# Layer 0's preparation: channel halves added before the averages, and the gate's second convolution in fours

## The chip, the cores and the metric

The kernel runs on one core of a Trainium2 chip. The metric is the device time of one launch in microseconds (us). The runs of the kernel before gave a median of 4865.72 us (4865.72 to 4866.03, three runs).

A core has five engines that work side by side, each through its own instructions in order: TensorE (PE, matmuls), VectorE (DVE), ScalarE (ACT), GpSimd (POOL), and SyncE (SP), which here only issues transfers. They wait for each other by semaphores. PE writes its results to PSUM, in banks of 128 partitions x 512 float32; the other data lie in SBUF, 128 partitions wide.

## What is computed

Two attention layers run one after the other on an image x of shape (2, 256, 64, 64): two batches, 256 channels, N = 4096 positions. Only the start of the first layer is touched. Cut to what matters:

```python
xf = x.reshape(B, C, N).transpose(0, 2, 1)
mu = mean(xf, axis=-1)                        # over the 256 channels
var = mean(square(xf - mu), axis=-1)
xn = (xf - mu) * rsqrt(var + LN_EPS) * norm_w + norm_b
q, k, v = split(einsum('bnc,oc->bno', xn, qkv_w))      # 4 heads of 16
attn = softmax(q k^T * 16**-0.5)
d1 = relu(einsum('oc,bchw->bohw', conv1_w, x) + conv1_b)   # 128 channels
dyn = einsum('oc,bchw->bohw', conv2_w, d1) + conv2_b       # 1 channel: the gate
out = (attn * dyn) v, projected by out_w
x1 = sigmoid(gamma * out + x)
```

The second layer is attention over x1 with 4 heads of 64, a projection, biases and the sum with x1.

## The kernel before

All products are in float32. The 256 channels are two halves of 128 partitions (CC = 2), so a tile of x is 128 x 2 x 512. A block is one such tile: 512 positions of one batch, and there are 16 of them (2 batches x 8).

The kernel has three large stages: the preparation of layer 0 for all blocks (the loop at L527), layer 0's main loop over 256 steps of scores, exponentials and weighted values, and layer 1. The preparation is what concerns us. Its loop runs over n = 0 to 18, and three blocks are in work at once: new (block n), middle (block n-1) and old (block n-2). The order in which one turn writes down its work is:

- prep_load (L264): x of blocks n and n+1, if it is not there already. These transfers are not bound to the order written down; they are issued as soon as one of the four buffers of x is free, and a buffer is freed by the first convolution of its block (prep_gate).
- prep_var (L287) of middle: two matmuls with mean_w, a 128 x 128 matrix filled with 1/256, one for each half of the squares, added up in a PSUM bank. Every partition then holds the variance. prep_std (L294) takes the root on ACT.
- prep_mean (L268) of new: two matmuls with the same matrix on the halves of x.
- prep_rstd (L299) of middle: the reciprocals on DVE, in four pieces of 128 columns, two before and two after the next step.
- prep_center (L276) of new: DVE subtracts the mean (xc), ACT squares it (sq).
- prep_norm (L303) of middle: three instructions on POOL, the product with the reciprocal and, for each half, scale and shift.
- first_maxima: four score matmuls of 32 x 128 (L394, tile a) whose row maxima DVE takes (L398); this is done twice in a turn, from n = 3 on, with four PSUM banks of its own.
- prep_product and prep_keep of old: q and k (L258, tile p), copied out by ACT.
- prep_gate of middle: the first convolution (L258, tile d1p), then ACT's relu into d1.
- prep_values (L335) of old: eight matmuls of 128 columns (L340, tile vp), and ACT's copy.
- prep_dyn (L363) of middle: one matmul with c2, a column of 128 weights, to one row of a bank (L365, tile dynp); prep_keep_dyn (L370) adds the bias on ACT into a 1 x 512 row and stores that row to the memory dyn0, from which the main loop later loads it for the block.

Nearly all of these are wrapped in `seq`, which keeps the order written down on every engine. Not wrapped are transfers, the constants, and fill_wpad (L134), six small DVE copies that lay out the q, k, v weights: these may be placed anywhere that their inputs allow. The preparation's products take their PSUM banks from four in rotation (prep_bank). clear_v (L242) zeroes v of one batch on POOL and writes its columns of ones, in turn 0 for batch 0 and in turn 6 for batch 1.

```python
for c in range(CC):                                   # prep_var
    seq(nc.tensor.matmul(ps, mean_w, sq[:, c, :], start=(c == 0), stop=(c == CC - 1)))
```

Of the kernel before, what the change touches and what calls it, by code (L numbers as in the profile page):

```python
# [8 lines left out]
F32 = mybir.dt.float32  # L9
BF16 = mybir.dt.bfloat16  # L10
AF = mybir.ActivationFunctionType
ALU = mybir.AluOpType
# [3 lines left out]
P = 128  # L16
NB = 512
C = 256
CC = C // P
# [8 lines left out]
def conv_attention_kernel(  # L28
# [19 lines left out]
    nc = tc.nc  # L48
    B, _, N = x.shape
# [17 lines left out]
    const_prep = own_prep.enter_context(tc.tile_pool(name="const_prep", bufs=1))  # L67
# [7 lines left out]
    dyn0 = [  # L75
        [dram.tile([1, NB], F32, tag=f"dyn0_{b}_{j}", name=f"dyn0_{b}_{j}") for j in range(NJ)]
        for b in range(B)
    ]
# [7 lines left out]
    def load_x(b, j, pool=xpool, tag="x"):  # L86
        t = pool.tile([P, CC, NB], F32, tag=tag, name=f"{tag}_{b}_{j}")
        nc.sync.dma_start(
            out=t, in_=x[b, :, bass.ts(j, NB)].rearrange("(c p) n -> p c n", p=P)
        )  # L90
        return t

    xs = {(0, 0): load_x(0, 0)}

    def const_load(shape, src, name, pool=const):
        t = pool.tile(shape, F32, tag=name, name=name)
        nc.scalar.dma_start(out=t, in_=src)
        return t
# [7 lines left out]
    c1 = const_load([P, CC, P], c1_wT.rearrange(by_chunk, p=P), "c1", const_prep)  # L106
    c1b = const_load([P, 1], c1_b, "c1b", const_prep)
    c2 = const_load([P, 1], c2_wT, "c2", const_prep)
    c2b = const_load([1, 1], c2_b, "c2b", const_prep)


    mean_w = const_prep.tile([P, P], F32, tag="mean_w", name="mean_w")
# [19 lines left out]
    make_identity(nc, ident)  # L132

    def fill_wpad():  # L134
        for s in range(3):
            for c in range(CC):
                nc.vector.tensor_copy(
                    wpad[s][:, c, :].rearrange("p (h e) -> p h e", e=32)[:, :, 1 : 1 + D0],
                    qkv_raw[:, c, s * H * D0 : (s + 1) * H * D0].rearrange(
                        "p (h d) -> p h d", d=D0  # L140
                    ),
                )
# [67 lines left out]
    seq = tc.keep_in_program_order  # L210
# [22 lines left out]
    with own0:  # L233
        prep = own_prep.enter_context(tc.tile_pool(name="prep", bufs=2))
# [7 lines left out]
        def clear_v(b):  # L242

            seq(nc.gpsimd.memset(vs0[b], 0.0))
            ones_at = vs0[b].rearrange("p m (h e) -> p m h e", e=32)[:, :, :, 0:1]
            seq(nc.gpsimd.memset(ones_at, 1.0))

        work, qs0, mxs, pts, avs, dyns, res, facts = {}, {}, {}, {}, {}, {}, {}, {}
# [4 lines left out]
        def prep_bank(name):  # L253
            return psw.tile([P, NB], F32, tag="bank", name=name)
# [9 lines left out]
        def prep_load(b, j):  # L264
            if (b, j) not in xs:
                xs[b, j] = load_x(b, j)

        def prep_mean(b, j):  # L268
            ps = prep_bank(f"mean_{b}_{j}")
            for c in range(CC):  # L270
                seq(nc.tensor.matmul(
                    ps, mean_w, xs[b, j][:, c, :], start=(c == 0), stop=(c == CC - 1)
                ))
            work["mean", b, j] = ps

        def prep_center(b, j):  # L276
            xc = prep.tile([P, CC, NB], F32, tag="xc", bufs=3, name=f"xc_{b}_{j}")
            sq = prep.tile([P, CC, NB], F32, tag="sq", bufs=1, name=f"sq_{b}_{j}")
            mean = work.pop(("mean", b, j))
            seq(nc.vector.tensor_tensor(  # L280
                xc, xs[b, j], mean.unsqueeze(1).to_broadcast([P, CC, NB]), ALU.subtract
            ))
            seq(nc.scalar.activation(sq, xc, AF.Square))
            work["xc", b, j] = xc
            work["sq", b, j] = sq

        def prep_var(b, j):  # L287
            ps = prep_bank(f"var_{b}_{j}")
            sq = work.pop(("sq", b, j))
            for c in range(CC):  # L290
                seq(nc.tensor.matmul(ps, mean_w, sq[:, c, :], start=(c == 0), stop=(c == CC - 1)))  # L291
            work["var", b, j] = ps

        def prep_std(b, j):  # L294
            std = prep.tile([P, NB], F32, tag="std", name=f"std_{b}_{j}")
            seq(nc.scalar.activation(std, work.pop(("var", b, j)), AF.Sqrt, bias=eps))
            work["std", b, j] = std

        def prep_rstd(b, j, i):  # L299
            std = work["std", b, j]  # L300
            seq(nc.vector.reciprocal(std[:, bass.ts(i, P)], std[:, bass.ts(i, P)]))
# [53 lines left out]
        def prep_gate(b, j):  # L355
            work["d1", b, j] = over_channels(prep_bank(f"d1p_{b}_{j}"), c1, xs.pop((b, j)))

        def prep_keep_gate(b, j):
            d1 = prep.tile([P, NB], F32, tag="d1", name=f"d1_{b}_{j}")
            seq(nc.scalar.activation(d1, work["d1", b, j], AF.Relu, bias=c1b))  # L360
            work["d1", b, j] = d1

        def prep_dyn(b, j):  # L363
            ps = prep_bank(f"dynp_{b}_{j}")
            seq(nc.tensor.matmul(  # L365
                ps[:1, :], c2, work.pop(("d1", b, j)), start=True, stop=True
            ))
            work["dyn", b, j] = ps

        def prep_keep_dyn(b, j):  # L370
            row = prep.tile([1, NB], F32, tag="dyn", name=f"dynrow_{b}_{j}")
            seq(nc.scalar.activation(
                row, work.pop(("dyn", b, j))[:1, :], AF.Identity, bias=c2b
            ))
            nc.sync.dma_start(out=dyn0[b][j], in_=row)

        def load_q(u):
            b, j = u
# [6 lines left out]
        def maxima(x, g):  # L385

            u = b, j = units0[x // NM]
            m, i = divmod(x % NM, PB)
            if u not in mxs:
                mxs[u] = small.tile([P, PB * H, NJ], F32, tag="mx0", name=f"mx0_{b}_{j}")  # L390
            for h in (2 * g, 2 * g + 1):
                r = slice(32 * h, 32 * h + 32)
                ps = bank(f"a0_{b}_{j}_{x % NM}_{h}")
                seq(nc.tensor.matmul(  # L394
                    ps, qs0[u][r, bass.ts(i, P)], kTs[b][r, bass.ts(m, NB)],
                    start=True, stop=True,
                ))
                seq(nc.vector.tensor_reduce(mxs[u][:, i * H + h, m : m + 1], ps, AX.X, ALU.max))  # L398
# [127 lines left out]
        blocks = [(b, j) for b in range(B) for j in range(NJ)]  # L526
        for n in range(len(blocks) + 3):  # L527

            def block(k):
                return blocks[n - k] if 0 <= n - k < len(blocks) else None  # L530

            def first_maxima(i):
                x = 2 * (n - 3) + i
                if 0 <= x < NM:
                    for g in (1, 0):
                        maxima(x, g)

            new, middle, old = block(0), block(1), block(2)
            if n == 0:
                clear_v(0)  # L540
            if n == 6:
                clear_v(1)
            if new is not None:
                prep_load(*new)
                if block(-1) is not None:
                    prep_load(*block(-1))
            if middle is not None:
                prep_var(*middle)
                prep_std(*middle)
            if new is not None:  # L550
                prep_mean(*new)
            if middle is not None:
                prep_rstd(*middle, 0)
                prep_rstd(*middle, 1)
            if new is not None:
                prep_center(*new)
            if n == 0:
                fill_wpad()
            if middle is not None:
                prep_rstd(*middle, 2)  # L560
                prep_rstd(*middle, 3)
                prep_norm(*middle)
            first_maxima(0)
            if old is not None:
                for s in range(2):
                    prep_product(*old, s)
                    prep_keep(*old, s)
            if middle is not None:
                prep_gate(*middle)
                prep_keep_gate(*middle)  # L570
            first_maxima(1)
            if old is not None:
                prep_values(*old)
                prep_keep_values(*old)
            if middle is not None:
                prep_dyn(*middle)
                prep_keep_dyn(*middle)
        own_prep.close()
        own_psum.close()
        own_psum = ExitStack()  # L580
# [48 lines left out]
    with (  # L629
# [389 lines left out]
        for n, u in enumerate(units):  # L1019
            b, g, j = u  # L1020
            t0 = n * US
            if n == 0:
                for i in range(NJ):
                    with_x(
                        t0 + KEYS_AT[i], "early", ("k", b, g, i), b, i,
                        lambda xt, b=b, g=g, i=i: keys(b, g, i, xt),
# [4 lines left out]
                        lambda xt, b=b, g=g, i=i: values(b, g, i, xt),  # L1031
# [142 lines left out]
        for j in range(NJ):  # L1174
            project_half(j, 1, last_att[0][:, bass.ts(j, NB)])
            nc.sync.dma_start(
                out=out[B - 1, :, bass.ts(j, NB)].rearrange("(c p) n -> p c n", p=P),
                in_=last_x[j],
# [50 lines left out]
```

## Time and profile before

| what | value |
|---|---|
| median of three runs | 4865.72 us |
| the profiled execution's own time | 4865.83 us |
| its span, first to last instruction | 4864.0 us |
| mean granted TensorE clock | 0.993 |
| preparation's first turns, until PE is busy without a gap | 0 to 35.59 us |
| preparation, to the last product of v | 238.5 us |
| first exponential of layer 0's main loop | 257.2 us |

One execution was recorded by the hardware profiler. A view gives for each group of instructions its line (L291 is line 291 of the kernel), its engine, what it writes and reads with the shape, a count, and its busy time; in brackets may stand how long the engine was idle before it, and on whom it waited. The chain of waits is followed back from the last instruction of the span, at each step to what released it; read in order of time it tells which engine set the pace in each stretch. Each float32 matmul shows as two records, and the ends of matmuls in a list overlap a little, since they are pipelined; the chain counts each piece of time once.

### The profile page before, as it was taken

To read this page: it belongs to the slowest core of one execution; us is meant where nothing else is said; L and a number is where in the kernel's file an instruction comes from. 1 tells how busy PE (TensorE), PEld (TensorE's weight loads), DVE (VectorE), ACT (ScalarE), POOL (GpSimd) and SP (SyncE) were. 2 spreads that over 40 slices of the span, in tenths; PEclk is the share of its full clock that TensorE was granted. 3 is DMA by queue.
4 is the path that set the end of the run, shared out by engine and by line. 5 is a ranking of instruction groups with operands and counts; after the bars stand their busy time and mean duration, and the time that the engine had idled before them with its cause. 6 is when DMAs were issued, how large, how long until landed. Compare 5 with 4: busy or idle time off the path is not lost.

```text
span 4864.0 us, 70477 instructions
## 1 busy us (share of the span) xinstructions
PE 4608.3 (95%) x27592; PEld 1517.7 (31%) x27592; DVE 3949.3 (81%) x4614; ACT 3418.6 (70%) x4547; POOL 2524.5 (52%) x1463
## 2 busy tenths in 40 slices
PE   9999999999999999879999999999999999999997
PEld 3433333333333333223232323222333333222222
DVE  5677777777777777218999999999998899999996
ACT  3356666666666666547888888888887788888884
POOL 3200000000000000007999999999998889999995
PEclk9999999999999999989999999999999999999999
DMA  3100000000000000021000110000102111100002
GB/s 96 38 1 16 14 14 14 14 17 14 14 14 16 21 12 12 7 67 55 22 25 22 41 40 25 22 24 27 55 27 63 49 56 40 31 7 14 14 18 70
DMA packets 105195, 139.57 MB, mean 29 GB/s; under 512 B 43742, under 2 KB 44574, under 8 KB 104750
## 3 DMA queue, kind: packets, MB, share of 16 engines
q1 hardware_dynamic: 103220, 134.61, 9.2%
q8 instruction: 216, 3.54, 0.3%
q14 instruction: 117, 0.96, 0.1%
q10 hardware_dynamic: 1642, 0.46, 0.0%
HBM read 93.33 MB, written 41.45 MB: 28 GB/s over the span
## 4 chain that ended last, share of the span: by engine, by line
PE 54%; POOL 18%; DVE 14%; issue 7%; ACT 6%; DMA 1%; ACTq 0%; POOLq 0%; DVEq 0%; SPq 0%
PE s L427 23%; POOL acc L878 16%; PE av L442 11%; DVE rmax L788 8%; PE s L771 5%; DVE raw L854 5%; ACT raw L789 3%; PE av L888 3%; ACT raw L866 2%; PE a L394 1%; POOL acc L876 1%; PE p L258 1%; PE k1p L670 1%; PE o L489 1%; PE var L291 1%
## 5 line engine op out<-in xcount | busy, mean ns | idle before, releaser
L878 POOL TENSOR_TENSOR acc<-acc,raw 128x1024 f32<-128x1024 f32 x886 | 2101.5, 2372 | 104.5 <-ACT raw L866 44.7
L398 DVE TENSOR_REDUCE mx<-a 128x1 f32<-128x512 f32 x2048 | 1311.6, 684 | 433.4 <-PE a L394 432.7
L430 ACT ACTIVATE p<-s 128x512 f32<-128x512 f32 x2048 | 1111.5, 595 | 725.6 <-PE s L427 371.6
L427 PE MATMUL s<-q,kT 32*128 32x512 f32 x4096 | 1252.4, 640 | 22.9 <-ACT p L430 22.9
L854 DVE TENSOR_TENSOR raw<-raw,shift 128x1024 f32<-128x1024 f32 x1024 | 1236.6, 1212 | 16.6 <-PE shift L849 9.6
L788 DVE TENSOR_TENSOR rmax<-s,rmax 128x1024 f32<-128x1024 f32 x960 | 1169.3, 1218 | 97.7 <-PE s L771 96.4
L771 PE MATMUL s<-q,k 64*128 64x512 f32 x4096 | 1111.7, 635 | 131.3 <-ACT raw L789 123.3
L789 ACT COPY raw<-s 128x1024 f32<-128x1024 f32 x1024 | 1036.1, 1012 | 270.1 <-DVE rmax L788 180.9
L866 ACT ACTIVATE raw<-raw 128x1024 f32<-128x1024 f32 x1024 | 1085.4, 1061 | 172.8 <-DVE raw L854 139.7
L394 PE MATMUL a<-kT,q 32*128 32x512 f32 x4096 | 1123.6, 643 | 1.4 <-DVE mx L398 1.3
L888 PE MATMUL av<-raw,v 128*64 128x512 f32 x4096 | 1000.4, 607 | 4.4 <-ACT raw L866 2.5
L483 POOL TENSOR_TENSOR f<-f,dyn 128x512 f32<-128x512 f32 x16 | 20.2, 1263 | 1444.9 <-ACT p L430 1294.7
L442 PE MATMUL av<-p,v 128*32 128x256 f32 (+1 forms) x7904 | 646.4, 399 | 0.0
L771 PEld LDWEIGHTS s<-q,k 64*128 64x128 f32 x4096 | 316.9, 185 | 810.1 <-ACT raw L789 609.4
L427 PEld LDWEIGHTS s<-q,kT 32*128 32x128 f32 x4096 | 403.9, 183 | 484.5 <-issue 366.2
L888 PEld LDWEIGHTS av<-raw,v 128*64 128x64 f32 x4096 | 243.6, 136 | 585.9 <-issue 423.4
L442 PEld LDWEIGHTS av<-p,v 128*32 128x32 f32 x7904 | 156.0, 108 | 748.6 <-issue 737.8
L394 PEld LDWEIGHTS a<-kT,q 32*128 32x128 f32 x4096 | 301.7, 184 | 29.7 <-DVE mx L398 17.5
L504 POOL TENSOR_SCALAR res<-res 128x1024 f32<-128x1024 f32 x16 | 16.7, 1045 | 400.5 <-ACT res L503 400.5
L876 POOL TENSOR_TENSOR acc<-raw,raw 128x1024 f32<-128x1024 f32 x64 | 152.2, 2378 | 99.4 <-ACT raw L866 99.4
L479 DVE RECIPROCAL f<-f 128x128 f32<-128x128 f32 x64 | 59.6, 939 | 96.2 <-ACT f L475 96.2
L808 DVE TENSOR_REDUCE negs<-rt 128x4 f32<-128x512 f32 x128 | 88.2, 689 | 50.3 <-PE rt L796 47.9
(323 smaller groups left out, 1946.1 us busy)
## 6 DMA issues: line engine op xcount, KB each, us to landing
x<-in_x_dram SPq DMA_DIRECT2D x16, 512.0 KB
res<-in_x_dram SPq DMA_DIRECT2D x16, 512.0 KB
x<-res SPq DMA_DIRECT2D x16, 512.0 KB
att<-rows SPq DMA_DIRECT2D x62, 128.0 KB
kd<-k1s SPq DMA_DIRECT2D x24, 256.0 KB
vd<-v1s SPq DMA_DIRECT2D x24, 256.0 KB
k<-kd SPq DMA_DIRECT2D x24, 256.0 KB
v<-vd SPq DMA_DIRECT2D x24, 256.0 KB
```

What stands on the lines that cost most here:

```text
L394: seq(nc.tensor.matmul(ps, qs0[u][r, bass.ts(i, P)], kTs[b][r, bass.ts(m, NB)], start=True, stop=True,))
L398: seq(nc.vector.tensor_reduce(mxs[u][:, i * H + h, m : m + 1], ps, AX.X, ALU.max))
L427: seq(nc.tensor.matmul(ps, kTs[b][r, bass.ts(m, P)], qs0[u][r, :], start=True, stop=True))
L430: seq(nc.scalar.activation(pt[:, k, :], ps, AF.Exp, scale=D0**-0.5))
L442: seq(nc.tensor.matmul(avs[u][32 * h : 32 * h + 32, cols], vs0[b][:, m, 32 * h : 32 * h + 32], pts[t, h // 2][:, h % 2, cols], start=(m == ...
L771: seq(nc.tensor.matmul(ps[:, k, :], ks[b, g, m // PB][r, bass.ts(m % PB, P)], qs1[u][r, :], start=True, stop=True,))
L788: seq(nc.vector.tensor_tensor(rmax[u, n], ps, before, ALU.max))
L789: seq(nc.scalar.copy(raw, ps))
L854: seq(nc.vector.tensor_tensor(raws[t], raws[t], shifts[u, t % NM // GS], ALU.add))
L866: seq(nc.scalar.activation(p, p, AF.Exp, scale=D1**-0.5))
L878: seq(nc.gpsimd.tensor_tensor(accs[u, n], accs[u, n], p, ALU.add))
L888: seq(nc.tensor.matmul(avs1[u, n][k * D1 : (k + 1) * D1, :], v[:, m % PB, k, :], raws[t][:, k, :], start=(m % GS == 0), stop=(m % GS == GS ...
```

## The change

The two halves of the channels are added elementwise before the average is taken, so that one matmul with mean_w gives the mean, and one the variance. A new function, prep_sum, adds the halves of x into a tile of 128 x 512, on POOL at the end of the turn before the block is new, and for block 0 on DVE in turn 0. prep_center adds the two halves of the squares on POOL, after ACT's Square.

The second convolution is no longer done for each block. Its weight column is repeated 32 times (c2rep, a DVE copy in fill_wpad), and in the turns n = 4, 8, 12 and 16 four blocks are done at once: four matmuls of 128 x 32, each to its own 32 partitions of one PSUM bank. One ACT instruction adds the bias to all 128 partitions, and four transfers store one row each. For this the tile d1 has five buffers instead of two, and the bias c2b is loaded to all partitions. The zeroing of v for batch 0 moves from turn 0 to turn 1.

```diff
--- before.py
+++ after.py
@@ -106,7 +106,8 @@
     c1 = const_load([P, CC, P], c1_wT.rearrange(by_chunk, p=P), "c1", const_prep)
     c1b = const_load([P, 1], c1_b, "c1b", const_prep)
     c2 = const_load([P, 1], c2_wT, "c2", const_prep)
-    c2b = const_load([1, 1], c2_b, "c2b", const_prep)
+    c2b = const_load([P, 1], c2_b.partition_broadcast(P), "c2b", const_prep)
+    c2rep = const_prep.tile([P, 32], F32, tag="c2rep", name="c2rep")
 
 
     mean_w = const_prep.tile([P, P], F32, tag="mean_w", name="mean_w")
@@ -132,6 +133,7 @@
     make_identity(nc, ident)
 
     def fill_wpad():
+        nc.vector.tensor_copy(c2rep, c2.to_broadcast([P, 32]))
         for s in range(3):
             for c in range(CC):
                 nc.vector.tensor_copy(
@@ -265,12 +267,16 @@
             if (b, j) not in xs:
                 xs[b, j] = load_x(b, j)
 
+        def prep_sum(b, j, engine=nc.gpsimd):
+
+            x = xs[b, j]
+            both = prep.tile([P, NB], F32, tag="both", name=f"both_{b}_{j}")
+            seq(engine.tensor_tensor(both, x[:, 0, :], x[:, 1, :], ALU.add))
+            work["both", b, j] = both
+
         def prep_mean(b, j):
             ps = prep_bank(f"mean_{b}_{j}")
-            for c in range(CC):
-                seq(nc.tensor.matmul(
-                    ps, mean_w, xs[b, j][:, c, :], start=(c == 0), stop=(c == CC - 1)
-                ))
+            seq(nc.tensor.matmul(ps, mean_w, work.pop(("both", b, j)), start=True, stop=True))
             work["mean", b, j] = ps
 
         def prep_center(b, j):
@@ -281,14 +287,15 @@
                 xc, xs[b, j], mean.unsqueeze(1).to_broadcast([P, CC, NB]), ALU.subtract
             ))
             seq(nc.scalar.activation(sq, xc, AF.Square))
+            squares = prep.tile([P, NB], F32, tag="squares", name=f"squares_{b}_{j}")
+            seq(nc.gpsimd.tensor_tensor(squares, sq[:, 0, :], sq[:, 1, :], ALU.add))
             work["xc", b, j] = xc
-            work["sq", b, j] = sq
+            work["sq", b, j] = squares
 
         def prep_var(b, j):
             ps = prep_bank(f"var_{b}_{j}")
             sq = work.pop(("sq", b, j))
-            for c in range(CC):
-                seq(nc.tensor.matmul(ps, mean_w, sq[:, c, :], start=(c == 0), stop=(c == CC - 1)))
+            seq(nc.tensor.matmul(ps, mean_w, sq, start=True, stop=True))
             work["var", b, j] = ps
 
         def prep_std(b, j):
@@ -356,23 +363,22 @@
             work["d1", b, j] = over_channels(prep_bank(f"d1p_{b}_{j}"), c1, xs.pop((b, j)))
 
         def prep_keep_gate(b, j):
-            d1 = prep.tile([P, NB], F32, tag="d1", name=f"d1_{b}_{j}")
+            d1 = prep.tile([P, NB], F32, tag="d1", bufs=5, name=f"d1_{b}_{j}")
             seq(nc.scalar.activation(d1, work["d1", b, j], AF.Relu, bias=c1b))
             work["d1", b, j] = d1
 
-        def prep_dyn(b, j):
-            ps = prep_bank(f"dynp_{b}_{j}")
-            seq(nc.tensor.matmul(
-                ps[:1, :], c2, work.pop(("d1", b, j)), start=True, stop=True
-            ))
-            work["dyn", b, j] = ps
-
-        def prep_keep_dyn(b, j):
-            row = prep.tile([1, NB], F32, tag="dyn", name=f"dynrow_{b}_{j}")
-            seq(nc.scalar.activation(
-                row, work.pop(("dyn", b, j))[:1, :], AF.Identity, bias=c2b
-            ))
-            nc.sync.dma_start(out=dyn0[b][j], in_=row)
+        def prep_dyn(four):
+
+            ps = prep_bank("dynp_{}_{}".format(*four[0]))
+            for i, u in enumerate(four):
+                seq(nc.tensor.matmul(
+                    ps[32 * i : 32 * i + 32, :], c2rep, work.pop(("d1", *u)),
+                    start=True, stop=True,
+                ))
+            rows = prep.tile([P, NB], F32, tag="dyn", bufs=1, name="dynrows_{}_{}".format(*four[0]))
+            seq(nc.scalar.activation(rows, ps, AF.Identity, bias=c2b))
+            for i, (b, j) in enumerate(four):
+                nc.sync.dma_start(out=dyn0[b][j], in_=rows[32 * i : 32 * i + 1, :])
 
         def load_q(u):
             b, j = u
@@ -536,7 +542,7 @@
                         maxima(x, g)
 
             new, middle, old = block(0), block(1), block(2)
-            if n == 0:
+            if n == 1:
                 clear_v(0)
             if n == 6:
                 clear_v(1)
@@ -544,6 +550,8 @@
                 prep_load(*new)
                 if block(-1) is not None:
                     prep_load(*block(-1))
+            if n == 0:
+                prep_sum(*new, nc.vector)
             if middle is not None:
                 prep_var(*middle)
                 prep_std(*middle)
@@ -572,9 +580,10 @@
             if old is not None:
                 prep_values(*old)
                 prep_keep_values(*old)
-            if middle is not None:
-                prep_dyn(*middle)
-                prep_keep_dyn(*middle)
+            if middle is not None and n % 4 == 0:
+                prep_dyn(blocks[n - 4 : n])
+            if block(-1) is not None:
+                prep_sum(*block(-1))
         own_prep.close()
         own_psum.close()
         own_psum = ExitStack()
```

## The prediction

> **What bounds the kernel now.** I read the page's header, then its chain of waits, then asked for that chain in order of time over the preparation, which is the only stage that the diff touches.
>
> ```profile
> span 4864.0 us, 70477 instructions
> PE 4608.3 (95%) x27592; PEld 1517.7 (31%) x27592; DVE 3949.3 (81%) x4614; ACT 3418.6 (70%) x4547; POOL 2524.5 (52%) x1463
> ```
>
> TensorE is busy 95% of the whole span, but that is a mean over several stages. The busy time of the engines by stage says more:
>
> ```profile
> 0.00:35.59 35.59, 24.72 (x57) 10.22 (x57) 11.67 (x17) 10.60 (x13) 16.75 (x37) 0.90 0.57 167
> 35.59:49.64 14.05, 14.05 (x55) 6.21 (x55) 9.33 (x13) 4.70 (x7) 3.87 (x3) 1.00 0.27 83
> 49.64:218.25 168.61, 168.61 (x649) 74.55 (x649) 111.91 (x156) 56.38 (x84) 50.12 (x38) 1.00 0.16 51
> 218.25:230.81 12.56, 12.56 (x54) 5.68 (x54) 8.21 (x12) 3.71 (x6) 3.86 (x3) 1.00 0.06 21
> 230.81:258.00 27.19, 25.01 (x101) 12.87 (x104) 18.74 (x31) 4.42 (x7) 0.00 (x0) 0.75 0.03 11
> ```
>
> Columns: stretch, its length, then busy time of PE, weight loads, DVE, ACT, POOL, then the granted clock. From 35.59 to 230.81 PE is busy for the entire stretch; DVE has 9.33 of 14.05 us, POOL 3.87. So this stage is PE alone, and its chain shows only PE, in a period of 14.05:
>
> ```profile
> 91.79 1.91 PE var L291 x4
> 93.70 1.72 PE mean L271 x4
> 95.42 1.07 PE a L394 x8
> 96.49 3.63 PE p L258 x8
> 100.12 1.72 PE d1p L258 x4
> 101.84 1.07 PE a L394 x8
> 102.91 1.98 PE vp L340 x16
> 104.89 0.95 PE dynp L365 x2
> 105.84 1.91 PE var L291 x4
> ```
>
> The counts are records, two to a matmul: mean is two matmuls, 0.86 us each. The same shape costs 1.72 after itself and 1.91 after dynp, so leaving the 1-column product costs 0.19. One more view, the timeline of one period (beginning at S = 105.84), gives the other engines:
>
> ```profile
> 108.57 1.76 DVE L301 RECIPROCAL std<-std 128x128 f32<-128x128 f32 x2 [3.16 <-ACT std L296]
> 110.25 1.16 DVE L280 TENSOR_TENSOR xc<-x,mean 128x1024 f32<-128x1024 f32 x1
> 111.33 1.75 DVE L301 RECIPROCAL std<-std 128x128 f32<-128x128 f32 x2
> 113.00 2.41 DVE L398 TENSOR_REDUCE mx<-a 128x1 f32<-128x512 f32 x4
> ...
> 111.51 1.06 ACT L283 ACTIVATE sq<-xc 128x1024 f32<-128x1024 f32 x1 [2.97 <-DVE xc L280]
> ...
> 113.23 2.34 POOL L306 TENSOR_TENSOR xc<-xc,std 128x1024 f32<-128x1024 f32 x1 [10.09 <-DVE std L301]
> 115.68 1.51 POOL L310 TENSOR_SCALAR xc<-xc,nw,nb 128x512 f32<-128x512 f32 x2
> ```
>
> The reader should see that POOL idles 10.09 us ahead of its work and DVE 3.16 ahead of its own, so both have room, but not twice as much.
>
> [...] four av products of 256 columns and 32 outputs each (L442) take 0.57 us in the chain, not four times 0.43. [...] POOL's 1024-element tensor_tensor takes 2346 ns here and 2372 (L878) beside a DVE busy nine tenths[...] (mean of block 0 takes 3.43 us, twice 1.72, and dynp after 3.28 us of idle takes 1.87, not 0.95).
>
> **PE's account.** Var and mean lose one matmul each per block: 2 x 0.86. The second convolution costs 0.95 + 0.19 for every block now, 4.56 for four; afterwards four products stand in four column groups. No row has them at 512 columns. From av: 2 x 0.43 + 0.14 = 1.00, plus 0.19 to leave the mode: 1.19 per four blocks. Bounds: 0.86 + 0.19 if perfectly side by side; 4 x 0.95 + 0.19 = 3.99 if one after the other. I take 1.19, as av shows the overlap. A period without it is 0.86 + 0.86 + 1.07 + 3.63 + 1.72 + 1.07 + 1.98 = 11.19; four periods 44.76 + 1.19 = 45.95, against 56.20.
>
> **Is the next engine late?** POOL gains two adds of 512 elements per block. The row nearest is L483, tensor_tensor 128x512, 1.26 us (half of L306 would be 1.17, the lower bound; 1.5 I take as the upper). All of these are in order on POOL: the squares' add of block n, the normalisation of n-1 (three instructions, 113.23 to 117.19 = 3.96), and the sum for n+1, which the mean of the next period waits for. With var shorter by 1.91 - 0.86 = 1.05, DVE's chain begins at S + 1.68; the subtraction at S + 110.25 - 105.84 - 1.05 = 3.36; Square ends at S + 5.68; squares S + 5.73 to 6.99 (the last reciprocal, S + 6.19, is earlier, so the normalisation is delayed by 0.8); normalisation to 10.95; sum to 12.2. The next period begins at S + 11.19 and wants its mean 0.86 later, 12.05. So PE waits about 0.2 us, and every second period, since a late mean moves the next var too: two periods are at least 12.25 + 0.86 + 9.47 = 22.58 instead of 22.38. Where four products were just inserted there is no wait. I count 0.4 per four periods: 46.35. What is queued behind the new waits: behind the squares' add stand the normalisation (needed by p only at S' + 2.8, done by S' - 0.2) and the sum; behind the waiting mean all of PE.
>
> DVE: its maxima begin at S + 6.11, the first four end at 8.5; the second group of a needs these four banks and cannot finish before 9.0, while PE itself gets through it at 9.21. Covered by 0.2; busy 9.33 of 11.6. ACT loses 12 row copies of 0.68; its widest piece, rows 128x512, costs as much as the 1x512 row. DMA: the 16 row stores are issued in four bunches by SP; x loads are issued when the first convolution frees a buffer, three blocks ahead (115.92, just after d1p), so the earlier need of x for the sum is hidden. Without that cover each would show its landing time. The zeroing of v for batch 1 (3.5 + 0.3 us on POOL) ends at about S + 5.1, before the squares' add. The later fold, layer 0's main loop and layer 1 keep their instructions and should merely be earlier.
>
> **Start.** Block 0's sum on DVE costs about 0.6 (half of 1.16, plus a start), mean one cold matmul less (1.72). But the DVE's subtraction still comes at 8.7, behind the wpad copies that wait for qkv_raw (landed 7.13). The new c2rep copy needs c2, issued 1.6 us after qkv_raw on the same queue: if it stands ahead of them, up to 1.9 us are lost, if behind, nothing; I take 0.8. Then: Square to 11.0, squares to 12.35, var (cold, 1.8) to 14.2, table load and std as now to 16.3, second subtraction 18.0 to 19.1, squares of 1 to 21.65, normalisation to 25.6, sum of 2 to 26.85. PE idles over 3 us twice, so it restarts cold: mean of 2 to 28.6, p to 33.1 (the first of its four matmuls cold), d1p 34.8, vp 36.8. Now that point is 35.59: 1.2 lost. The next period takes 11.2 instead of 14.05, giving 1.6 gained at 49.64, 0.8 with the c2rep share. A warm PE would make it 2.8, a cold one with the full c2rep wait -0.3.
>
> **Sum.** Twelve periods (49.64 to 218.25): 168.6 - 3 x 46.35 = 29.5. The period at 218.25 (no mean): 12.56 becomes 12.56 - 1.05 - 0.95 + 1.00 = 11.56, gain 1.0. With the start's 0.8: 31.3. Against the profiled execution: 4864.0 - 31.3 = 4832.7 span, with 1.8 around it (4865.83) 4834.5; the median before, 4865.72, lies 0.1 below that execution.
>
> **Rivals.**
> (a) More is gained: POOL is never late (adds at 1.17), PE stays warm at the start. 29.5 + 1.2 + 1.0 + 2.8 = 34.5, to 37 with perfect packing and a start without idle time: about 4830. For it: PE's account alone. Against: POOL's margin is -0.15 us.
> (b) Less is gained. POOL's adds at 1.5 us push the sum by 0.5, which costs about 0.25 to 0.5 per period, 3 to 6 in twelve; if the four products run one after another, 2.8 x 4 = 11.2 more. Together about 15 to 28 left, near 4845 at the middle. For it: tight margins on POOL; against: L442 shows packing.
> (c) No change: the removed work was hidden. The stretch with PE at 14.05 of 14.05 excludes it unless POOL takes the same period: about 4866.
> (d) Slower: POOL becomes the bound. The loop squares, normalisation, sum, mean crosses two periods; POOL's share is 1.26 + 3.96 + 1.26 = 6.48 of 22.58. It reaches 28.1, the old pace, if that share grows by 5.5, that is, if POOL is 1.85 times slower [...]. At twice, two periods are 29.1, 14.5 each: 12 x 0.5 = 6 us plus about 6 in the start, some 4878. Against: the 2346 and 2372 ns above.
>
> **How the numbers follow.** Forecast (25 to 34 gained) 0.62, (a) 0.10, (b) 0.17, (c) 0.05, (d) 0.06. The range leaves out (c), (d), the worse half of (b) and little of (a): 4828 to 4847. About 0.2%, 9.7 us, is what can be told from no change: faster 0.89, within it 0.05, slower 0.06.
>
> **What would show it.** PE's period at 11.2 to 11.6 with a 0.1 to 0.4 us wait of mean on POOL in some periods; a dynp group of about 1.0 us every fourth; POOL's adds near 1.26; the start of layer 0's main stage (the first p exponentials, now 257.2) near 226. I am wrong if the adds are far longer beside DVE, if PE's clock falls below 1.00 after 50 us, if mean waits longer than 0.5 us in each period, or if what is gained by then is given back in a later stage.

## The result, and the profile after

| | before | changed |
|---|---|---|
| median | 4865.72 us | 4832.43 us (4831.76 to 4837.02, four runs) |
| ratio to before, 95% interval | 1 | 0.9935 [0.9917, 0.9952] |
| span of the profiled execution | 4864.0 us | 4829.9 us |
| PE busy in the span | 4608.3 us | 4571.5 us |
| start of the turn n = 4 | 49.64 us | 47.84 us |
| start of the turn n = 16 | 218.25 us | 190.83 us |
| fold: DVE begins to reduce the row maxima of the main loop's first unit of work (negmax) | 244.56 us | 216.08 us |
| from the fold to the end | 4619.5 us | 4613.9 us |

33.3 us less by the medians; 4834.5 was predicted, with a range of 4828 to 4847. The fold is the first instruction behind the preparation that is easy to find in every trace, so the table splits the time there. Of the 34.1 us between the two spans 28.5 lie ahead of it and 5.6 behind it, where the change leaves every instruction as it was. Both parts need an explanation.

First the busy time of the engines by stage of the changed kernel (stretch, its length, busy us of PE, weight loads, DVE, ACT, POOL, then the granted clock, the DMA share and GB/s):

```profile
0.00:36.22 36.22, 20.88 (x43) 9.09 (x44) 11.79 (x19) 9.65 (x11) 24.02 (x43) 0.91 0.53 147
36.22:47.84 11.62, 11.62 (x50) 5.58 (x49) 9.24 (x13) 3.98 (x6) 5.83 (x5) 1.00 0.36 127
47.84:190.83 142.99, 142.99 (x601) 67.22 (x601) 111.92 (x157) 49.87 (x75) 78.88 (x62) 1.00 0.19 62
190.83:202.32 11.49, 11.49 (x59) 5.11 (x57) 8.30 (x13) 3.43 (x6) 3.86 (x3) 1.00 0.06 24
```

Twelve periods fell from 168.61 to 142.99 us, POOL's busy time rose from 50 to 79 us, DVE's 112 us stayed. PE is again busy for the whole stretch, and it would be easy to conclude that PE alone sets the pace. The chain of waits in order of time (start, us, what) says something else:

```profile
95.50 0.86 PE var L298 x2
96.36 0.86 PE mean L279 x2
97.22 1.07 PE a L400 x8
98.29 3.63 PE p L260 x8
101.92 1.72 PE d1p L260 x4
103.64 1.50 PE a L400 x7
105.14 1.98 PE vp L347 x16
107.12 0.99 PE dynp L374 x8
108.11 0.63 PE var L298
```

Var and mean cost one matmul each, as they should; the four products stand side by side in 0.99. But the second group of scores takes 1.50 us where the first takes 1.07: a period is 11.62 us, not 11.19. The timeline of the same period (start, length, engine, line, what; in brackets the idle time ahead, and on whom) shows ACT, DVE and POOL beside it:

```profile
96.40 0.69 ACT L303 ACTIVATE std<-var,eps 128x512 f32<-128x512 f32 x1 [0.47 <-PE var L298]
...
97.12 1.76 DVE L308 RECIPROCAL std<-std 128x128 f32<-128x128 f32 x2 [1.53 <-ACT std L303]
98.80 1.16 DVE L286 TENSOR_TENSOR xc<-x,mean 128x1024 f32<-128x1024 f32 x1
99.88 1.75 DVE L308 RECIPROCAL std<-std 128x128 f32<-128x128 f32 x2
101.55 2.42 DVE L404 TENSOR_REDUCE mx<-a 128x1 f32<-128x512 f32 x4
104.73 2.48 DVE L404 TENSOR_REDUCE mx<-a 128x1 f32<-128x512 f32 x4 [0.76 <-PE a L400]
...
101.19 1.26 POOL L291 TENSOR_TENSOR squares<-sq 128x512 f32<-128x512 f32 x1 [5.20 <-ACT sq L289]
102.41 2.34 POOL L313 TENSOR_TENSOR xc<-xc,std 128x1024 f32<-128x1024 f32 x1
104.86 1.52 POOL L317 TENSOR_SCALAR xc<-xc,nw,nb 128x512 f32<-128x512 f32 x2
106.34 1.27 POOL L274 TENSOR_TENSOR both<-x 128x512 f32<-128x512 f32 x1
```

The fourth of the first maxima ends at 103.97, and so frees the last of the four score banks only after the group's first matmul began (103.57). The group ends 1.17 us behind that moment. Its four matmuls run side by side: the first three began within 0.02 us of each other, at 103.57. The last one, let in at 104.02, had its whole length of 1.12 us still to go. PE's busy time hides this, since the others are running meanwhile. So one period is a ring, a round of steps each of which waits for the one before: var, ACT's root at 96.40, DVE without a gap from 97.12 to 103.97, the last score to 105.14, vp to 107.12, and then the next turn. POOL's adds take 1.26 to 1.27 us, as L483 had said.

### The profile page after: what moved, and what is told of

Same layout as the page of the kernel before. It is cut to its first block, busy times and chain, and to the rows that moved or that the text cites. A ratio compares the mean times of both kernels' runs of the same rounds, so it can differ in the third digit from the quotient of the medians.

```text
span 4829.9 us, 70386 instructions
## 1 busy us (share of the span) xinstructions
PE 4571.5 (95%) x27528; PEld 1505.4 (31%) x27528; DVE 3949.2 (82%) x4616; ACT 3412.2 (71%) x4535; POOL 2563.0 (53%) x1494
## 4 chain that ended last, share of the span: by engine, by line
PE 52%; POOL 19%; DVE 14%; issue 7%; ACT 6%; DMA 1%; SPq 0%; ACTq 0%; POOLq 0%; DVEq 0%
PE s L433 23%; POOL acc L887 17%; PE av L448 12%; DVE rmax L797 9%; DVE raw L863 5%; PE s L780 5%; ACT raw L798 3%; PE av L897 3%; ACT raw L875 2%; PE a L400 2%; PE p L260 1%; POOL acc L885 1%; PE k1p L679 1%; PE o L495 1%; PE vp L347 1%
```

## The experiments

Two theories for the 1.50. A: the wait for the bank of the fourth maximum. B: PE's own cost at this place, or POOL. A third, C, is about the 5.6 us behind the fold: that stretch has no fixed length, and differs between executions of one program. The diffs below are extracts where "..." stands or where the text says so.

**One more bank for the scores, one less for the preparation's products.**

```diff
-        psx = own_psum.enter_context(tc.tile_pool(name="psx", bufs=4, space=PSUM))
-        psw = own_psum.enter_context(tc.tile_pool(name="psw", bufs=4, space=PSUM))
+        psx = own_psum.enter_context(tc.tile_pool(name="psx", bufs=5, space=PSUM))
+        psw = own_psum.enter_context(tc.tile_pool(name="psw", bufs=3, space=PSUM))
```

> Five PSUM banks for the score matmuls instead of four, three for the preparation instead of four. Theory A: in the changed kernel's steady period of 11.62 us the second group of scores takes 1.50 instead of 1.07 us because its fourth matmul waits for the bank that DVE's fourth maximum frees, and then still takes its own 0.86. With a fifth bank it waits for the third, which is 0.6 us earlier: the group returns to about 1.07 to 1.1 us, the period to 11.2 to 11.3 (PE's own sum is 11.19; the mean may wait up to 0.1 for POOL), and twelve periods give 4 to 5 us: about 4828. Theory B (rival): the 0.43 us is a cost of PE itself at this place, or comes from POOL; then the period stays 11.62 and the time 4832. With only three banks the preparation could also wait anew; that would show as idle PE before a product.

Measured: 4830.29 us, ratio 0.9927 [0.9912, 0.9942], above the expected 4828; the fold at 211.52, 4.6 us earlier than in the changed kernel. Its chain, from a turn with a late mean:

```profile
92.72 1.24 POOL both L274
93.95 0.04 issue
94.00 1.13 PE mean L279 x2
95.12 1.07 PE a L400 x8
96.19 3.63 PE p L260 x8
99.83 1.72 PE d1p L260 x4
101.54 1.07 PE a L400 x8
102.61 1.98 PE vp L347 x16
```

The second group is back at 1.07: theory A holds, B falls. And now POOL's sum stands in the chain ahead of mean, which is the wait that the prediction had counted on; twelve periods take 139.75 us (var at 46.53 to var at 186.28), against 139.05 in the prediction's account. That is 3.2 us less than in the changed kernel, where 4 to 5 were expected, since the waits for POOL take some of it back. The other 1.3 us of the 4.6 lie in the start, and prove nothing: the start alone differed by 1.2 us between two executions of the changed kernel, while the twelve periods repeated to 0.01 us. Less of the gain is seen in the median (2.1 us) than at the fold; more on that below.

**The same, and the sum moved ahead of the squares' add, so that POOL does it a period earlier than needed.**

```diff
+            if block(-1) is not None:
+                prep_sum(*block(-1))
             if new is not None:
                 prep_center(*new)
...
-            if block(-1) is not None:
-                prep_sum(*block(-1))
```

> As e1, and the sum of the halves for the next block stands before the squares' add on POOL, not behind the normalisation. Theory A: no mean waits for POOL any more, so the period is 11.19 us (12.38 with the four products). In the start the mean of block 2 (at 25.1 us in the changed kernel, behind POOL's normalisation of block 0) comes earlier, by up to 3 us for the point where p of block 0 begins (27.2). Altogether about 4.9 plus 1 to 3.3 us less than the changed kernel: 4824 to 4827. Rival: the start is bound by the normalisation that p waits for (it ends at 23.8) and by the cold clock, and gives less than 1 us: about 4827 to 4828.

Measured: 4827.0 us (4822.78 to 4828.06), ratio 0.9917 [0.9901, 0.9934]; the fold at 204.98, 11.1 us ahead of the changed kernel's. The period in its chain, by PE alone, 88.00 to 99.19, is 11.19, and twelve periods take 137.85 us, which is PE's account without any wait (12 x 11.19 + 3 x 1.19):

```profile
88.00 0.86 PE var L298 x2
88.86 0.86 PE mean L279 x2
89.72 1.07 PE a L400 x8
...
96.14 1.07 PE a L400 x8
97.21 1.98 PE vp L347 x16
99.19 0.99 PE dynp L374 x8
```

The start gives more than expected: the turn n = 4 begins at 42.05 instead of 47.84 us, since block 2's mean no longer waits behind POOL's normalisation, and p of block 0 begins at 23.66 instead of 27.19. This is the fastest version that was run.

**The halves alone**: the second convolution for each block, as before (an extract: the two functions themselves are again those of the kernel before).

```diff
-            if middle is not None and n % 4 == 0:
-                prep_dyn(blocks[n - 4 : n])
+            if middle is not None:
+                prep_dyn(*middle)
+                prep_keep_dyn(*middle)
```

> The second convolution for each block alone, as before; the halves are added as in the change. Theory A: the product stands behind the values, outside of the loop from var through DVE's maxima to the scores, so it adds its whole 0.95 + 0.19 to a period of 11.62: 12.76 us, twelve periods 153.1 instead of 143.0 us, time about 4842.5. Rival: the 0.43 us wait shrinks because the longer period gives DVE time: 11.19 + 1.14 = 12.33, time about 4837.5.

Measured: 4846.46 us, ratio 0.9960 [0.9945, 0.9974]; the fold at 228.27, 16.3 us ahead of the kernel before. A turn, from its chain:

```profile
49.76 1.05 PE var L298 x2
...
58.09 1.50 PE a L401 x7
59.59 1.98 PE vp L347 x16
61.57 0.95 PE dynp L372 x2
62.52 1.05 PE var L298 x2
```

The period is 12.76 as theory A said, not 12.33 (twelve take 153.12 us): the second convolution stands behind vp, outside of the ring up to the scores, so it adds its whole time and gives DVE no more room. The median is 4 us above the expected 4842.5; in the profiled execution the turn n = 4 began 1.9 us later than in the changed kernel, and the stretch behind the fold was 4.4 us longer.

**The fours alone**: mean and variance with two matmuls, no adds on POOL, and v of batch 0 zeroed in turn 0 again (an extract; mean is changed in the same way).

```diff
-            seq(nc.tensor.matmul(ps, mean_w, sq, start=True, stop=True))
+            for c in range(CC):
+                seq(nc.tensor.matmul(ps, mean_w, sq[:, c, :], start=(c == 0), stop=(c == CC - 1)))
```

> Only the second convolution in fours; mean and variance with two matmuls each, as before. By PE's account a period falls from 14.05 to 12.91 us (no product, no mode change), 1.19 more in every fourth: 52.83 for four, 158.5 for twelve periods instead of 168.6. With the three first turns about 12 us come out of the preparation: the eight maxima that end it (at 239.67 us before, 211.19 changed) begin at 227 to 228.5. If the parts are independent, this and what e3 kept (16.3 us) make up the whole 28.5. Rival: DVE's chain, not PE, already sets a period of 12.9; then it stays near 13.3 and less than 8 us come out. Time about 4853, with the 3 us by which runs of one kernel differ.

Measured: 4852.27 us (nine runs), ratio 0.9978 [0.9967, 0.9988]; the maxima at 225.68 and the fold at 230.57, 14.0 us ahead of the kernel before.

```profile
85.87 1.72 PE var L293 x4
87.59 1.72 PE mean L273 x4
...
95.72 1.07 PE a L395 x8
96.79 1.98 PE vp L342 x16
```

Twelve periods are 158.45 us, against 158.5 expected, and the group of scores takes 1.07: with two more matmuls in a period DVE is in time. So the bank wait comes with the halves: it is there with the halves alone (1.50) and not with the fours alone. The maxima came 1.3 us earlier than the expected 227, because the start was shorter (the turn n = 4 at 45.96). At the fold 14.0 and 16.3 make 30.3, of which 28.5 are seen. In the twelve periods the two parts add up: 10.16 and 15.49 make 25.65, and 25.62 are seen. What does not add up lies in the start, which differs by more than a us between executions anyway.

**The sum twice**, to find out how much room POOL has left.

```diff
-            seq(engine.tensor_tensor(both, x[:, 0, :], x[:, 1, :], ALU.add))
+            for _ in range(1 if (b, j) == (0, 0) else 2):
+                seq(engine.tensor_tensor(both, x[:, 0, :], x[:, 1, :], ALU.add))
```

> The sum of the halves is computed twice on POOL (from block 1 on), only to double this one cost. Theory A, by the two-period account of the prediction: the sum ends 12.11 us after the period's start now, the mean wants it at 11.62 + 0.86 = 12.48, so POOL has 0.37 us to spare; another 1.23 us makes the mean late, and two periods become 12.11 + 1.23 + 0.05 + 0.86 + 9.47 = 23.7, 11.86 each instead of 11.62, about 3 us in twelve periods, and 1 to 2 more in the start: 4835.5 to 4837.5. Rival: POOL is idle for 5.2 us of a period and takes it in without a trace: 4832.5.

Measured: 4841.09 us, ratio 0.9948 [0.9933, 0.9963], above the expected 4835.5 to 4837.5; twelve periods 147.37 instead of 143.00. PE's timeline, mean in a late turn:

```profile
97.93 1.02 PE L299 MATMUL var<-squares,mean_w 128*128 128x512 f32 x2
99.98 1.12 PE L280 MATMUL mean<-both,mean_w 128*128 128x512 f32 x2 [1.03 <-POOL both L275]
```

POOL has no room for one more add, though it idles over 5 us in a period of the changed kernel: the idle time stands ahead of the squares' add, the work behind it. Late and punctual turns alternate, 12.49 and 11.63; the account had 23.7 for the pair and the trace has 24.1, because the punctual turn still has the bank wait. That and 1.7 us in the start are 6.1 at the fold; the rest of the difference in the medians lies behind it.

**The second group of scores behind vp**, a way to cover the bank wait without a bank.

```diff
-            first_maxima(1)
             if old is not None:
                 prep_values(*old)
                 prep_keep_values(*old)
+            first_maxima(1)
```

> The changed kernel with the second group of scores behind the product of v instead of ahead of it; four banks as in the change. Theory A: the fourth score matmul waits for the bank of DVE's fourth maximum, which is free 8.5 us after the period's start; the product of v is now done first, and PE reaches the group at about 10.1, so nothing waits: the group takes 1.07 us, the period 11.2 to 11.4 (the mean may wait for POOL up to 0.2, and DVE's last maxima now end only about 0.3 us after the reciprocals of the next period could begin). Gain in twelve periods 3 to 5 us, as in e1: the eight maxima at 206 to 208 us. Rival (a cost of PE itself where it changes its mode): 1.50 us stay, and the period is 11.62.

A miss: 4838.4 us, ratio 0.9949 [0.9934, 0.9964], the fold at 219.77, 3.7 us later than in the changed kernel. Its chain:

```profile
93.24 1.07 PE a L400 x8
94.31 1.05 PE var L298 x2
95.37 0.01 issue
95.38 1.12 PE mean L279 x2
96.50 1.48 PE a L400 x7
```

The second group takes 1.07 now, which again speaks against a cost of PE itself, but the first has the 1.48: its banks hold scores that DVE has only just received. DVE's four maxima ended at 96.81, and the group ends at 97.98, again 1.17 us behind. The wait changed places. Twelve periods are 143.46 us. The start was 1.2 us shorter than in the first trace of the changed kernel, and the last turns take 4.5 us more (from var of the turn n = 16 at 189.88 to the fold 29.9 us, against 25.4): at the end DVE has twelve maxima left (from 212.01), where it had eight (from 211.17).

**Two idle matmuls, and four, in the last turn**, meant as a delay, to see whether the stretch behind the fold keeps its length.

```diff
+            if n == len(blocks) + 2:
+                ps = prep_bank("idle")
+                for _ in range(2):
+                    seq(nc.tensor.matmul(ps, ident, kTs[0][:, :NB], start=True, stop=True))
```

> The changed kernel, with two matmuls of 128x128x512 whose result nobody reads behind the last product of v: a delay of 1.72 us at the end of the preparation, otherwise nothing. Theory C: what lies behind the preparation is not of fixed length. TensorE's clock falls to half in windows at the pauses after the preparation and between the layers, and how many fall depends on the moment at which a pause is reached (half clock after the preparation, by the trace's clock record: 58.0 us before, 44.4 us changed; the stretch behind the eight maxima 4624.3 and 4618.7 us). Then the time moves by anything from -3 to +6 us, not by 1.7, and the stretch behind the maxima goes with the time at half clock, some 0.35 us for each us. Rival: the stretch is fixed, and the 5.6 us belong to the change; then the time is 4832.4 + 1.7 = 4834.1, with the stretch at 4618.7.

> As e6 with four such matmuls, 3.44 us. Theory C: the time moves by something between -1 and +8 us, and the stretch behind the eight maxima goes with the time at half clock as in e6. Rival: 4832.4 + 3.4 = 4835.8, the stretch behind the maxima 4618.7 us as in the changed kernel.

They delayed nothing that lasts. PE began them in a pause in which it waits for DVE's maxima (fold at 215.90 and 214.94); the next scores came later (217.88 instead of 216.10 with two), but the first score of the main loop began at 225.2 and 226.0 us, against 225.7 in both traces of the changed kernel. The clock's record shows 3.4 us at half clock around this pause in each of the two, against 10.2 and 17.1. So they don't serve as a delay. As further traces they do: 4832.28 and 4833.88 us, ratios 0.9937 [0.9922, 0.9951] and 0.9941 [0.9926, 0.9955], with 4613.6 and 4619.6 us behind the fold.

**Second traces of three kernels**, unchanged.

> The changed kernel once more, for a second trace. Theory C: the stretch behind the preparation (from the instruction that folds the first maxima, at 216.08 us in the first trace, to the end: 4613.8 us with 44.4 us at half clock) differs between executions of one and the same program, by up to 6 us, and goes with the time at half clock by 0.3 to 0.4 us for each us; the fold itself stays within 1.5 us of 216.1, since only the start knows a cold clock. Rival: the stretch is a property of the changed program; then it is 4613.8 again within 1 us, whatever the clock's record says.

> The kernel before once more, for a second trace (first: fold at 244.56 us, stretch behind it 4619.4 us with 58.0 us at half clock). Theory C: fold at 243 to 246, the stretch between 4613 and 4622, on the same line against the time at half clock as the changed kernel's. Rival: 4619.4 within 1 us.

> The kernel of e2 once more (first: fold at 204.98 us, stretch behind it 4621.3 us with 64.9 us at half clock, the longest of all traces). Theory C: the stretch comes out shorter, 4613 to 4621, with less time at half clock; the fold stays at 204 to 206. Rival: it stays 4621, as a price that the shorter preparation pays later.

Measured, with all other traces. The time at half clock is that which the trace's clock record gives between the preparation and the end, without the last slow stretch, which the end of the trace cuts off. The last two columns belong to one pause, explained below the table.

| trace | span, us | fold at | from fold to end | half clock in it | most of the pause in one window | half clock after the pause |
|---|---|---|---|---|---|---|
| before, first | 4864.0 | 244.56 | 4619.5 | 58.0 | 1.72 | 0 |
| before, second | 4863.0 | 243.04 | 4619.9 | 58.0 | 1.56 | 0 |
| changed, first | 4829.9 | 216.08 | 4613.9 | 44.4 | 1.62 | 0 |
| changed, second | 4834.7 | 214.88 | 4619.8 | 61.4 | 2.51 | 6.8 |
| five banks | 4828.7 | 211.52 | 4617.1 | 58.0 | 1.71 | 0 |
| early sum, first | 4826.3 | 204.98 | 4621.3 | 64.9 | 2.37 | 6.8 |
| early sum, second | 4823.1 | 205.09 | 4618.0 | 54.6 | 1.74 | 0 |
| halves alone | 4846.6 | 228.27 | 4618.3 | 54.6 | 2.03 | 6.8 |
| fours alone | 4850.3 | 230.57 | 4619.8 | 61.4 | 2.80 | 3.4 |
| sum twice | 4840.3 | 222.16 | 4618.1 | 54.6 | 1.91 | 6.8 |
| later maxima | 4837.8 | 219.77 | 4618.1 | 58.0 | 2.50 | 6.8 |
| idle 2 | 4829.5 | 215.90 | 4613.6 | 47.8 | 1.61 | 0 |
| idle 4 | 4834.5 | 214.94 | 4619.6 | 58.0 | 1.95 | 6.8 |

The changed kernel itself has 4613.9 us in one execution and 4619.8 in another. The rival is out: a difference of 5.6 us there needs no change of the kernel. The early sum shows the same, with 4621.3 and 4618.0 us. The kernel before repeated itself within 0.4 us, with the same time at half clock, so the expectation of a scatter there was not put to the test by it. The stretch grows with the time at half clock, by some 0.3 to 0.4 us for each us (44.4 to 64.9: 7.4 us more). Where it goes can be seen by the busy time of the two executions of the changed kernel at the join of the layers. First execution:

```profile
2100.00:2130.00 30.00, 15.55 (x33) 5.25 (x32) 0.75 (x1) 6.08 (x8) 1.04 (x1) 0.83 0.59 197
...
2180.00:2200.00 20.00, 20.00 (x118) 11.05 (x116) 15.86 (x15) 15.27 (x18) 16.57 (x7) 1.00 0.26 81
```

Second execution:

```profile
2100.00:2130.00 30.00, 15.61 (x33) 5.25 (x32) 0.75 (x1) 5.74 (x8) 1.04 (x1) 0.81 0.60 196
...
2180.00:2200.00 20.00, 20.00 (x96) 10.97 (x98) 13.47 (x12) 13.62 (x16) 13.46 (x6) 0.84 0.22 71
```

PE is half idle from 2100 to 2130 in both. Afterwards the first execution runs at full clock (1.00) and gets 118 matmul records done in 20 us; the second is at 0.84 and has 96. The pauses are those of the kernel before as well. The half clock in the last stretch follows a pause in which PE waits for ACT. Its end in the first and in the second execution:

```profile
2179.58 1.13 PE L780 MATMUL s<-q,k 64*128 64x512 f32 x4 [2.94 <-ACT raw L798]
...
2179.90 2.08 PE L780 MATMUL s<-q,k 64*128 64x512 f32 x4 [2.94 <-ACT raw L798]
```

All 13 traces have this pause, 2.93 or 2.94 us long. In each of them the edges of the slow stretches lie on one grid of 3.413 us, to within 0.01 us, so the windows of this grid can be counted through the trace and laid over the pause; that gives the last two columns. In the seven traces in which 1.91 us or more of the pause fell into one window, the clock was halved from that window's end on; in the six with 1.74 us or less it was not. The changed kernel and the early sum each have both. So for this pause the moment at which it is met does decide. For the longer pauses ahead of it (6.9 and 10 us) the number of slow windows differs too, and what decides it there stays open.

## Why the prediction was right, by its own steps

- **PE sets the pace of the preparation**: right in the kernel before. With the fours alone all that was removed from PE came out of the period (14.05 to 12.91); with the halves all but the 0.43 us of the bank wait.
- **Var and mean, 0.86 each**: right, as measured in each chain.
- **Four products in 1.00 plus 0.19**: measured 0.99, with all four begun within 0.02 us (at 107.05), and var behind them 1.06 instead of 0.86, so 0.20. What the prediction and the expectations call the mode stands here only for such extra time: 0.20 here, and 0.19 for var behind dynp in the kernel before (1.91 against the 1.72 of mean behind var). ACT's row for all four blocks, 128x512, took 0.69, where the 1x512 row had taken 0.68.
- **POOL's adds at 1.26**: right, 1.26 to 1.27. DVE's 2.42 for four maxima and 1.75 for two reciprocals are as before (2.41 and 1.75), and so is POOL's product of 128x1024 (2.34), so neither engine was seen to slow the other.
- **PE waits about 0.2 us for POOL's sum in every second period**: it did not in the changed kernel, since the period of 11.62 gives POOL 0.4 us more. Where the period was 11.19 (five banks) the wait came, and the twelve periods agreed within 0.7 us with the account.
- **"The second group of a needs these four banks and cannot finish before 9.0, while PE itself gets through it at 9.21. Covered by 0.2"**: this is the step that failed. The 9.0 let the last matmul finish half a group after the bank came free. It finishes 1.17 us after: 9.64 behind the period's start (105.14 - 95.50). So the period is set by the ring through DVE, 11.62 us long, and twelve periods gave 25.6 instead of 29.5 us: 12 x 0.43 = 5.2 lost, less the 1.2 of waits for POOL that were counted and did not come.
- **The start, 0.8**: measured 1.8. The c2rep copy was placed behind the wpad copies (7.94 us), so its share of 0.8 wasn't lost. DVE's subtraction came at 8.03, not at 8.7. ACT's table load for the root ran at 10.35 us, ahead of var's end, and not behind it as in the kernel before (14.78), which took it off the path; so block 2's mean, waiting for POOL's sum as foreseen, began at 25.1 instead of 26.85. Part of that went again: behind 4.03 us of idle time ahead of this mean PE had a granted clock of 0.50 from 25.00 to 31.28, and q and k of block 0 took 5.5 us where 4.5 were reckoned. PE without a gap began at 36.22, 0.6 later than before instead of 1.2, and the next period gave 2.4 instead of 2.85. Of this 1.8 itself more than one us is not firm: the turn n = 4 began 1.2 us earlier in the second trace of the changed kernel, and 1.5 in that of the kernel before.
- **The turn n = 16, 1.0**: 12.56 to 11.49, 1.1.
- **Sum, 31.3**: 1.8 + 25.6 + 1.1 = 28.5 at the fold. The median's 33.3 is more than that; for the profiled execution the trace shows why, a short stretch behind the fold, while for the other runs of that median there is no trace. In the second traces of both kernels the whole difference is 28.3 us. Over every run of the two kernels on record (25 and 5) the medians are 31.7 us apart. So the predicted time was hit more closely than its account deserves, and that closeness is luck: the twelve periods were taken 4 us too favourably, and a stretch that differs by up to 6 us between executions returned it. That the gain lies within 25 to 34 us is no luck, as the fold shows. The main loop's first exponential came at 227.6, where near 226 was given as a sign.
- **Rival (d), POOL as the bound**: no. But the mechanism is there: one more add of 1.26 us per period costs 4.4 us in twelve (the sum twice).

## What to carry to other kernels

Where a bank is freed by the other engine, count the whole length of the last consumer behind that moment: here four matmuls ran side by side, but the last one to be let in still took its full 1.12 us and ended 1.17 us behind it, and PE showed as busy throughout. When work is taken from the engine that sets the pace, lay out the next ring to its end before believing the new period, and put work that is needed only in the next turn ahead of the waits of this one, as the early sum on POOL. When kernels differ by some us in 5000, compare them at a point behind the changed stage, not only at the end.

## What was not expected of the hardware

The length of 4600 us of unchanged work differed by 6 us (4613.9 and 4619.8) between two executions of the same program, along with 44.4 and 61.4 us at half clock. The slow stretches in the record are multiples of one window of 3.41 us (3.41, 6.83, 10.24, 13.65, 27.3 us, among others). The prediction reckoned with a slow restart where PE idles over 3 us, as dynp of block 0 before took 1.87 us instead of 0.95 behind 3.28 us of idle time. Here less was enough: a pause of 2.94 us was followed by half clock in seven traces of 13, where at least 1.91 us of it lay in one window (in the second execution of the changed kernel from 2179.5 on, for 6.8 us, while PE was busy again).
